# Second layer of a two-layer state-space kernel: eight convolution taps on VectorE, weights by tanh instead of sigmoid, short pieces read out of whole chunks; output stages with earlier loads and two square roots

## The chip, the cores and the metric

The kernel runs on one core of one Trainium2 chip, in fp32. The metric is the device time of one launch in microseconds (us). Engines are named as in the profile: PE is TensorE's matmul, PEld its weight load, DVE VectorE, ACT ScalarE, POOL GpSimd, SP the queue that issues most transfers.

## The reference, cut to what matters

The input is four images of 64x64 pixels with 192 channels. Two layers follow each other, both with 384 inner channels and 16 states. The first layer is a selective scan in four directions, with a layer norm, a gate silu(z), an output matmul and a residual. The change leaves all of it but its output stage alone. The second layer is a 3x3 depthwise convolution with a silu, and four scans of a different form:

```
xc = silu(depthwise_conv3x3(x_val) + conv_b)
dt = softplus(dt @ W_dt + b_dt)
log_dA = dt * A                              # A = -exp(A_log), per channel and state
log_decay = cumsum(log_dA)
decay = exp(log_decay)
h = decay * cumsum(dt * B * u / (decay + 1e-12))
y = sum over states of h * C, plus u * D     # rows, rows backward, columns, columns backward
out = x + (layernorm(y1 + y2 + y3 + y4) * silu(z)) @ W_out
```

A decay falls without limit along a row of pixels, so that a state's part of y is zero in fp32 from some pixel on. The weight decay / (decay + 1e-12) in the scans equals sigmoid(log_decay + ln 1e12), and it equals (1 + tanh((log_decay + ln 1e12) / 2)) / 2.

## The kernel before, in words

**Sizes.** An image is L = 4096 pixels, in NCH = 8 chunks of LC = 512; ND = 3 groups of 128 inner channels; KD = 4 directions; NJ = 4 blocks of 128 pixels in a chunk; NS = 16 states.

**Order of the whole.** The four images go through the first layer one after the other, each with its own projection, scans and output stage. Then the second layer takes all four together through `project`, `prepare`, `scans` and `finish`, each stage in full before the next. `finish` is one function for both layers: it is called four times with one image, and once with four.

**Who orders the instructions.** In both layers' scans the order on PE, ACT, DVE and POOL is written out by hand; SP's is set by a scheduler. In `project`, `prepare` and `finish` a scheduler orders all engines, bounded by the buffers of each pool.

**The output stage** (`finish`, from line 853). For each image, `stats` loads eight y tiles (L870 on), takes mean and variance of each pixel on DVE (L875, L876), and after all eight one square root on ACT and one reciprocal (L878, L879) for all 32 groups of 128 pixels. Then for each of eight tiles: load of the gate zg (L887), Silu on ACT (L888), load of the residual xl, normalisation of four blocks on DVE (L894), 12 transposes on PE (L901) into PSUM, read by ACT with gamma and beta into v (L904), the product v·zg on POOL (L907), 12 output matmuls on PE (L912; each shows as two records), the residual added on DVE (L915) and a store (L916). After the fifth tile of an image the next image's `stats` begin.

**Projection of the second layer** (`project`, from line 1005). For each image and channel group: in-projection matmuls into pad (L1040); for each half of the image, tap 0 on ACT (L1052), tap 1 on ACT into a tile of its own (L1053), their sum on POOL (L1054), and taps 2 to 8 on DVE (L1056), each 128x2048. Then a silu on ACT (L1057); six copies on POOL of the first pixels of each direction into uc (L1064, L1067); 16 matmuls by the diagonal D (L1074), their copies on ACT (L1078) and stores to y. At the image's end uc is stored (L1084), and the gate is projected and stored (L1088).

**What is scanned** (classes, line 947). Since decays end early, a direction's first 256 pixels are enough for state 0, 128 for states 1 to 3, 64 for states 4 to 7 and 32 for states 8 to 15. So each image has chunks of 512 columns for the four directions together: M (the first 128 pixels of each direction), E (the next 128, state 0 only), and two short pieces of M: S (first 64) and Q (first 32). Backward directions have theirs at the other end. A test for the limits leads to a full-length second path, which is not executed with these inputs.

**Preparation** (`prepare`, from line 1092). For M and then E of each image: load uc (L1189), three matmuls to xd (L1192, L1194), three to dp (L1110), softplus as max(dp, 0) + ln(1 + exp(-|dp|)): Abs and Exp on ACT (L1117, L1118), four POOL steps over 128x1536 (L1121, L1122, L1123, L1125), Ln on ACT between (L1124), the sum on DVE (L1127) with dp computed again. Then cumulative sums of dt, the test, e = dt·u (L1199), and `keep` (from L1163), which stores to DRAM: C's rows, B turned, e turned, dt and cum. For the short pieces POOL copies parts of dt, cum, e and of xd into small tiles (L1212, L1215), and `keep` is called for each of them too.

**Scans** (`scans`, from line 1219). Nine items per image: four of M with one state each, two of S with two states side by side, one of E, two of Q with four states. An item is: weights by Sigmoid on ACT (L1254) from cum, decays by Exp on ACT (L1267) from dt, B's product on ACT (L1287), x turned back on PE (L1302), x times weight (L1309) and the scan (L939) on DVE, times C on POOL (L1325), and the sum over states into PSUM by PE (L1343). Sigmoid and Exp lie in different tables of ACT, so weights are made in bursts of five and four items, with a table load before and after (L1254, L1410). Chunks of the next image are loaded at items 3, 5, 6 and 9. At item 2 of the next image the sums of an image are read out (L1369) and added to y in DRAM by DMAs with an add, issued by POOL (L1377, L1380).

Of the kernel before, what the change touches and what calls it, by code (L numbers as in the profile page):

```python
# [10 lines left out]
F32 = mybir.dt.float32  # L11
# [8 lines left out]
LC = 512  # L20
# [382 lines left out]
class FirstLayer:  # L403
# [449 lines left out]
    def finish(self, batches):  # L853

        nc, tc = self.tc.nc, self.tc
        with ExitStack() as ctx:
            pool = lambda name, bufs, **k: ctx.enter_context(tc.tile_pool(name=name, bufs=bufs, **k))
            py, pl, ps, pw = pool("fy", 12), pool("fl", 3), pool("fs", 2), pool("fw", 2)
# [6 lines left out]
            def stats(y):  # L865

                yts = []
                mv = ps.tile([128, NCH * NJ, 2], F32, name="mv")
                for t in range(NCH):
                    yt = py.tile([128, NJ, DI], F32, name="yt")  # L870
                    nc.sync.dma_start(yt, pos(y, t))
                    yts.append(yt)
                    st = pw.tile([128, NJ, nc.vector.BN_STATS_DIM], F32, name="st")
                    for j in range(NJ):
                        nc.vector.bn_stats(st[:, j, :], yt[:, j, :])  # L875
                        nc.vector.bn_aggr(mv[:, t * NJ + j, :], st[:, j, :])  # L876
                rs = ps.tile([128, NCH * NJ], F32, name="rs")
                nc.scalar.activation(rs, mv[:, :, 1], AF.Sqrt, bias=self.ln_eps)  # L878
                nc.vector.reciprocal(rs, rs)  # L879
                return yts, mv, rs  # L880

            ready = stats(batches[0][2])
            for b, (src, dst, _, gate) in enumerate(batches):
                yts, mv, rs = ready
                for t in range(NCH):
                    zg = pl.tile([128, ND, LC], F32, name="zg")
                    nc.sync.dma_start(zg, gate[t])  # L887
                    nc.scalar.activation(zg, zg, AF.Silu)  # L888
                    xl = pl.tile([128, NJ, CH], F32, name="xl")
                    nc.sync.dma_start(xl, pos(src, t))  # L890
                    yt = yts[t]
                    for j in range(NJ):
                        i = t * NJ + j
                        nc.vector.tensor_scalar(  # L894
                            yt[:, j, :], yt[:, j, :], mv[:, i, 0:1], rs[:, i : i + 1], ALU.subtract, ALU.mult
                        )
# [10 lines left out]
                    nc.gpsimd.tensor_tensor(v, v, zg, ALU.mult)  # L907
# [9 lines left out]
                    if t == NCH // 2 and b + 1 < len(batches):  # L917
                        ready = stats(batches[b + 1][2])


class Chunk:
# [3 lines left out]
    def __init__(self, name, width, dram, b):  # L925
        self.name, self.width = name, width
        kept = {"dt": [128, ND, width], "cum": [128, ND, width], "dtuT": [128, width // 128, DI]}
        kept |= {"bT": [128, width // 128, NS], "rows": [NS, width]}
        self.dram = {n: dram.tile(shape, F32, name=f"{n}{name}{b}") for n, shape in kept.items()}
# [12 lines left out]
class SecondLayer(FirstLayer):  # L942
# [6 lines left out]
    def __init__(self, tc, ctx, consts, w, dram, alive):  # L949
# [18 lines left out]
        nc.vector.tensor_scalar_mul(self.A, self.A, -1.0)  # L968
        self.A_max = wp.tile([128, len(self.CLASSES), ND], F32, name="A_max_s")
# [8 lines left out]
        nc.vector.memset(self.ln_q, LN_1E12)  # L978
# [13 lines left out]
    def run(self, batches):  # L992
# [4 lines left out]
        for b, uc in enumerate(ucs):  # L997
            kinds = (("M", LC), ("E", LC), ("S", LC // 2), ("Q", LC // 4))
            chunks.append([Chunk(name, width, self.dram, b) for name, width in kinds])
# [5 lines left out]
    def project(self, batches):  # L1005
        nc, tc = self.tc.nc, self.tc
        with ExitStack() as ctx:
# [17 lines left out]
            for b, (_, y, gate, uc_dram) in enumerate(batches):  # L1025
# [7 lines left out]
                for e in range(ND):  # L1033
# [12 lines left out]
                    for q in range(2):  # L1046
# [6 lines left out]
                        nc.scalar.activation(u, part(1), AF.Identity, scale=weight(1))  # L1053
                        nc.gpsimd.tensor_tensor(acc, acc, u, ALU.add)  # L1054
                        for tap in range(2, 9):
                            nc.vector.scalar_tensor_tensor(acc, part(tap), weight(tap), acc, ALU.mult, ALU.add)  # L1056
# [4 lines left out]
                        for r in range(2):  # L1061
                            k, row = (0, r * n) if q == 0 else (2, nh - (r + 1) * n)
                            to = uc[:, r, e, k * SEG : (k + 1) * SEG].rearrange("p (h w) -> p h w", w=HW)
                            nc.gpsimd.tensor_copy(to, u[:, row : row + n, :])  # L1064
                            for k, col in ((1, r * n), (3, HW - (r + 1) * n)):
                                to = uc[:, r, e, k * SEG : (k + 1) * SEG].rearrange("p (w h) -> p w h", h=HW)
                                nc.gpsimd.tensor_copy(to[:, :, q * nh : (q + 1) * nh], wide[:, col : col + n, :])  # L1067
# [24 lines left out]
    def prepare(self, ucs, batches):  # L1092
        nc, tc = self.tc.nc, self.tc
        with ExitStack() as ctx:
# [63 lines left out]
            def starts(t, n):  # L1158

                v = t.rearrange("... (h k w) -> ... h k w", h=2, w=SEG)  # L1160
                return [v[..., 0, :, :n], v[..., 1, :, SEG - n :]]

            def keep(chunk, xd, tiles):  # L1163

                nb = chunk.width // 128
                nc.sync.dma_start(chunk.dram["rows"], xd[48:64, : chunk.width])
                bp = ps_x.tile([128, NJ, NS], F32, name="bp", tag="xp")
                for j in range(nb):
                    nc.tensor.transpose(bp[:, j, :], xd[32:48, j * 128 : (j + 1) * 128], ident[32:48, 32:48])
                bT = p3.tile([128, NJ, NS], F32, name="bT")  # L1170
                nc.vector.tensor_copy(bT[:, :nb], bp[:, :nb])
                nc.sync.dma_start(chunk.dram["bT"], bT[:, :nb])
                dtuT = p2.tile([128, NJ, DI], F32, name="dtuT")
                for j in range(nb):
                    tp = ps_t.tile([128, DI], F32, name="tp")
                    for d in range(ND):
                        nc.tensor.transpose(
                            tp[:, d * 128 : (d + 1) * 128], tiles["e"][:, d, j * 128 : (j + 1) * 128], ident
                        )
                    nc.scalar.copy(dtuT[:, j, :], tp)  # L1180
                nc.sync.dma_start(chunk.dram["dtuT"], dtuT[:, :nb])
                for name in ("dt", "cum"):
                    nc.sync.dma_start(chunk.dram[name], tiles[name][:, :, : chunk.width])

            for uc_dram, (main, ext, *parts) in zip(ucs, batches):
                before = None
                for r, chunk in enumerate((main, ext)):
# [15 lines left out]
                    tiles = {"dt": dt, "cum": cum, "e": e}  # L1203
                    keep(chunk, xd, tiles)
                    for part in parts if r == 0 else ():
                        n = part.width // KD
                        own = {}
                        for name, t in tiles.items():
                            own[name] = p2.tile([128, ND, LC // 2], F32, name=f"{name}_p")
                            for to, of in zip((slice(0, 2 * n), slice(2 * n, 4 * n)), starts(t, n)):  # L1210
                                to = own[name][:, :, to].rearrange("p d (k w) -> p d k w", w=n)
                                nc.gpsimd.tensor_copy(to, of)  # L1212
                        xo = p2.tile([NX, LC // 2], F32, name="xd_p")
                        for to, of in zip((slice(0, 2 * n), slice(2 * n, 4 * n)), starts(xd[32:64], n)):
                            nc.gpsimd.tensor_copy(xo[32:64, to].rearrange("p (k w) -> p k w", w=n), of)  # L1215
                        keep(part, xo, own)


    def scans(self, batches, ys):
        nc, tc = self.tc.nc, self.tc  # L1220
        with ExitStack() as ctx:
            pool = lambda name, bufs, **k: ctx.enter_context(tc.tile_pool(name=name, bufs=bufs, **k))
            p1, p2, p3, p4, p6 = (pool(f"s{b}", b) for b in (1, 2, 3, 4, 6))
# [15 lines left out]
            def load(it):  # L1239
                for name, shape in (("dt", [128, ND]), ("cum", [128, ND]), ("dtuT", [128]), ("bT", [128])):  # L1240
                    t = p1.tile(list(it.dram[name].shape), F32, name=f"{name}{it.name}")
                    nc.sync.dma_start(t, it.dram[name])
# [4 lines left out]

            def weight(g):

                it, states, _ = flat[g]  # L1250
# [307 lines left out]
```

## Time and profile before

| | us |
|---|---|
| median of 3 runs (lowest, highest) | 11562.15 (11552.21, 11568.8) |
| profiled execution, its span | 11574.44, 11572.7 |
| four images of the first layer, each | about 2484 |
| of this the output stage, first load to last store | 90.3, 86.8, 89.9, 89.8 |
| second layer's projection, first tap to last | 10003.2 to 10617.6 |
| its preparation | 10640 to 10875 |
| its scans | 10875 to 11262 |
| its output stage | 11264 to 11573 |
| DVE, ACT, PE, POOL busy over the span | 84%, 84%, 83%, 79% |
| granted TensorE clock, mean | 0.924 |

A row of an instruction group gives: line, engine, operation, out<-in, partitions x elements, count; then busy us and mean ns of one; then the engine's idle time just before them and what ended most of it. "A<-B" in that last part reads: the engine waited for line B's engine. A row by window gives each engine's busy time, the granted clock, the share of the DMA engines' time and GB/s.

### The profile page before, as it was taken

How to read it: one execution, taken by the hardware profiler on the slowest of the kernel's cores; microseconds unless marked ns; L12 is line 12 of the kernel's file. 1: busy time of each engine (PE TensorE's matmuls, PEld its weight loads, DVE VectorE, ACT ScalarE, POOL GpSimd, SP SyncE). 2: the span in 40 equal slices, each digit the busy share in tenths (PEclk: the TensorE clock that was granted, in tenths of full speed). 3: DMA queues.
4: the chain of work that ended last, by engine and by line, in shares of the span. 5: the costliest groups of instructions: out<-in, count | busy, mean ns of one | idle time of the engine just before them, and what ended most of it. 6: DMA issues, size and time to landing. Idle time of an engine off the chain costs nothing. (4 is left out here: it accounts for less than half of the span.)

```text
span 11572.7 us, 172113 instructions
## 1 busy us (share of the span) xinstructions
PE 9631.2 (83%) x61497; PEld 7333.9 (63%) x61497; DVE 9684.7 (84%) x11675; ACT 9692.9 (84%) x16786; POOL 9137.6 (79%) x3024
## 2 busy tenths in 40 slices
PE   8998888878988888779988888789888888677567
PEld 4776666656776666657766666557766666444346
DVE  4999899957999899939998999669998999675456
ACT  5999999948999999849999999579999999454564
POOL 3999899937999899829998999559998999454444
PEclk8999999988999999989999999889999999887688
DMA  4433344444333344443333444443333443423446
GB/s 124 108 104 100 93 100 100 97 138 111 111 103 95 96 100 99 112 133 109 108 99 93 100 98 100 125 125 107 102 100 94 99 100 92 128 97 127 145 121 224
DMA packets 802422, 1277.16 MB, mean 110 GB/s; under 512 B 56954, under 2 KB 485511, under 8 KB 801044
## 3 DMA queue, kind: packets, MB, share of 16 engines
q1 hardware_dynamic: 796692, 1259.76, 39.6%
q0 software_dynamic: 4864, 6.29, 0.4%
q8 instruction: 489, 8.01, 0.3%
q14 instruction: 377, 3.09, 0.1%
HBM read 958.19 MB, written 307.69 MB: 109 GB/s over the span
## 5 line engine op out<-in xcount | busy, mean ns | idle before, releaser
L738 POOL TENSOR_TENSOR h<-h,bct 128x1536 f32<-128x1536 f32 x2048 | 7061.9, 3469 | 586.4 <-DVE carry L734 483.1
L724 DVE TENSOR_TENSOR_SCAN h<-a,carry,x 128x512 f32<-128x512 f32 x5376 | 6605.2, 1266 | 233.2 <-PE x L716 188.4
L716 PE MATMUL x<-ident,xT 128*128 128x128 f32 x24576 | 4004.7, 287 | 814.4 <-DVE h L724 712.9
L699 ACT ACTIVATE xT<-dtuT,bT 128x384 f32<-128x384 f32 x8192 | 4357.6, 609 | 94.7 <-PE x L716 89.6
L716 PEld LDWEIGHTS x<-ident,xT 128*128 128x128 f32 x24576 | 2807.3, 145 | 2139.4 <-DVE h L724 926.0
L711 ACT ACTIVATE a<-dt,A_log_f 128x512 f32<-128x512 f32 x6144 | 3976.5, 715 | 0.0
L751 PE MATMUL yp<-ident,h 128*128 128x128 f32 x24576 | 3705.9, 277 | 9.2 <-POOL h L738 9.1
L751 PEld LDWEIGHTS yp<-ident,h 128*128 128x128 f32 x24576 | 2946.4, 144 | 78.8 <-issue 63.6
L615 PE MATMUL dp<-xd,w_dtb_f 13*128 13x512 f32 x1536 | 889.9, 663 | 208.9 <-DVE dt L644 207.8
L724 DVE TENSOR_TENSOR_SCAN h<-a,x 128x512 f32<-128x512 f32 x768 | 899.2, 1207 | 195.2 <-PE x L716 117.6
L628 POOL TENSOR_SCALAR wl<-e 128x1536 f32<-128x1536 f32 x128 | 189.2, 1478 | 702.7 <-ACT e L624 379.5
L490 PE MATMUL pp<-xT,w_in 96*128 96x512 f32 x1152 | 551.7, 631 | 27.6 <-ACT pad L1040 26.2
L907 POOL TENSOR_TENSOR v<-v,zg 128x1536 f32<-128x1536 f32 x64 | 238.2, 3742 | 422.2 <-ACT v L904 380.3
L1056 DVE SCALAR_TENSOR_TENSOR acc<-pad,conv_w_s,acc 128x2048 f32<-128x2048 f32 x168 | 446.2, 2702 | 139.1 <-POOL acc L1054 138.8
L615 PEld LDWEIGHTS dp<-xd,w_dtb_f 13*128 13x128 f32 x1536 | 238.7, 192 | 453.9 <-DVE dt L644 336.6
L745 PE MATMUL yp<-yold,ident 128*128 128x512 f32 x768 | 444.0, 663 | 72.6 <-DMA yold<-y 72.6
L621 ACT ACTIVATE e<-dp 128x512 f32<-128x512 f32 x384 | 224.7, 585 | 311.3 <-DVE dt L644 141.8
L641 POOL TENSOR_TENSOR e<-e,wl 128x1536 f32<-128x1536 f32 x128 | 444.9, 3476 | 0.3
L638 POOL TENSOR_TENSOR e<-e,dt 128x1536 f32<-128x1536 f32 x128 | 442.5, 3457 | 0.3
L490 PEld LDWEIGHTS pp<-xT,w_in 96*128 96x128 f32 x1152 | 227.5, 203 | 295.5 <-issue 253.9
L912 PE MATMUL op<-w_out,v 128*128 128x192 f32 x1536 | 302.0, 364 | 105.9 <-POOL v L907 104.3
L734 DVE TENSOR_REDUCE carry<-h 128x3 f32<-128x3 f32 x2048 | 322.7, 158 | 70.4
(180 smaller groups left out, 7053.6 us busy)
## 6 DMA issues: line engine op xcount, KB each, us to landing
bct<-xp SPq DMA_DIRECT2D x1024, 512.0 KB, 5.0
uT<-uT SPq DMA_DIRECT2D x64, 768.0 KB, 4.8
yold<-y SPq DMA_DIRECT2D x64, 768.0 KB, 8.0
y<-yt SPq DMA_DIRECT2D x64, 768.0 KB, 4.2
uT<-uT SPq DMA_DIRECT2D x128, 384.0 KB, 5.0
yold<-y SPq DMA_DIRECT2D x128, 384.0 KB, 5.4
y<-yt SPq DMA_DIRECT2D x128, 384.0 KB, 4.6
yt<-y SPq DMA_DIRECT2D x64, 768.0 KB, 7.9
```

What stands on the lines that cost most here:

```text
L490: self.tc.nc.tensor.matmul(pp, self.w_in[:, i, e * 128 : (e + 1) * 128], self.xT[:, i, t * LC : (t + 1) * LC], start=(i == 0), stop=(i == ...
L615: nc.tensor.matmul(self.dp[d], w, self.xd[0 : DR + 1, :], start=True, stop=True)
L638: nc.gpsimd.tensor_tensor(self.e, self.e, self.dt, ALU.subtract)
L641: nc.gpsimd.tensor_tensor(self.e, self.e, self.wl, ALU.add)
L699: nc.scalar.mul(xTs[g][:, j, :], it.dtuT[:, j * DI : (j + 1) * DI], it.bT[:, j, n : n + 1])
L711: nc.scalar.activation(as_[g][:, d, :], it.dt[:, d, :], AF.Exp, scale=scale)
L716: nc.tensor.transpose(xs[g, d][:, j * 128 : (j + 1) * 128], xTs[g][:, j, d * 128 : (d + 1) * 128], ident)
L724: nc.vector.tensor_tensor_scan(along(hs[g][:, d, :], it.k), along(as_[g][:, d, :], it.k), along(xs.pop((g, d)), it.k), 0.0 if it.first els ...
L738: nc.gpsimd.tensor_tensor(hs[g], hs[g], bc(cs[g - n % 2][:, n % 2, :], 1, ND), ALU.mult)
L745: nc.tensor.matmul(it.yp[b], ident, yo, start=True, stop=False, skip_group_check=True)
L751: nc.tensor.matmul(it.yp[b][:, i * 128 : (i + 1) * 128], hs[g][:, d, j * 128 : (j + 1) * 128], ident, start=False, stop=n == NS - 1, is_tr ...
L1056: nc.vector.scalar_tensor_tensor(acc, part(tap), weight(tap), acc, ALU.mult, ALU.add)
```

## The change

It has four parts.

1. **Output stages.** `start` issues the loads of y and of the gate in turn, with the Silu of each gate tile; the gate has ten buffers of its own. Statistics, square root and reciprocal are split: tiles 0 and 1, then 2 to 7. Normalisation moves to POOL, all of it inside `start`; the product v·zg moves to DVE. `start` for the next image is called where `stats` was.
2. **Projection.** Tap 1 becomes a DVE tap; ACT's tap 1 and POOL's add go. The six copies into uc move from POOL to ACT.
3. **Preparation.** Only M and E are prepared and kept. POOL's copies and the short pieces' `keep` are gone. B turned is stored with a factor 0.5.
4. **Scans.** Weights by Tanh, with A and ln 1e12 halved, and the scan's first step is (tanh + 1)·x in one DVE instruction. Tanh and Exp share one table, loaded once; each item's weight is made one item ahead, beside its decay. For items of four states, three POOL multiplies of 128x512 by A come first, and one ACT instruction over 128x1536 instead of twelve. The chunks S and Q are read in pieces from M's arrays in DRAM: for dt and cum six transfers each, for e turned and B four each; C's rows by four. The chunks of the next image are loaded at items 4, 6, 7 and 8, three buffers hold weights (six before) and five hold h (four before). PE adds the first item of an image at item 3, and the read-out follows the scans of item 2.

Core of the diff (lines are after.py's and before.py's without numbers):

```diff
-            py, pl, ps, pw = pool("fy", 12), pool("fl", 3), pool("fs", 2), pool("fw", 2)
+            py, pz, pl, ps, pw = pool("fy", 10), pool("fz", 10), pool("fl", 3), pool("fs", 2), pool("fw", 3)
...
+            def start(y, gate):
+                yts, zgs = [], []
                 for t in range(NCH):
                     yt = py.tile([128, NJ, DI], F32, name="yt")
                     nc.sync.dma_start(yt, pos(y, t))
                     yts.append(yt)
+                    zg = pz.tile([128, ND, LC], F32, name="zg")
                     nc.sync.dma_start(zg, gate[t])
                     nc.scalar.activation(zg, zg, AF.Silu)
+                    zgs.append(zg)
+                for lo, hi in ((0, 2), (2, NCH)):
...
+                    nc.scalar.activation(rs, mv[:, :, 1], AF.Sqrt, bias=self.ln_eps)
+                    nc.vector.reciprocal(rs, rs)
+                    for t in range(lo, hi):
+                        for j in range(NJ):
+                            i = (t - lo) * NJ + j
+                            part = yts[t][:, j, :]
+                            nc.gpsimd.tensor_scalar(part, part, mv[:, i, 0:1], rs[:, i : i + 1], ALU.subtract, ALU.mult)
...
-                    nc.gpsimd.tensor_tensor(v, v, zg, ALU.mult)
+                    nc.vector.tensor_mul(v, v, zg)
...
-                        nc.scalar.activation(u, part(1), AF.Identity, scale=weight(1))
-                        nc.gpsimd.tensor_tensor(acc, acc, u, ALU.add)
-                        for tap in range(2, 9):
+                        for tap in range(1, 9):
                             nc.vector.scalar_tensor_tensor(acc, part(tap), weight(tap), acc, ALU.mult, ALU.add)
...
-                            nc.gpsimd.tensor_copy(to, u[:, row : row + n, :])
+                            nc.scalar.copy(to, u[:, row : row + n, :])
...
-                                nc.gpsimd.tensor_copy(to[:, :, q * nh : (q + 1) * nh], wide[:, col : col + n, :])
+                                nc.scalar.copy(to[:, :, q * nh : (q + 1) * nh], wide[:, col : col + n, :])
...
-                nc.vector.tensor_copy(bT[:, :nb], bp[:, :nb])
+                nc.vector.tensor_scalar_mul(bT, bp, 0.5)
...
+            def by_state(g, of, to, func, scale=1.0, bias=0.0):
                 it, states, _ = flat[g]
+                w = HALF // len(states)
+                if len(states) == 4:
+                    lo, hi = states[0], states[-1] + 1
+                    for d in range(ND):
+                        nc.gpsimd.tensor_tensor(
+                            halves(to[:, d, :]).rearrange("p h (n w) -> p h n w", w=w),
+                            bc(halves(of[:, d, :]), 2, hi - lo),
+                            bc(bc(self.A[:, 0, d, lo:hi], 1, 2), 3, w),
+                            ALU.mult,
+                        )
+                    nc.scalar.activation(to, to, func, scale=scale, bias=bias)
+                    return
...
+            def weight(g):
+                sg[g] = p3.tile([128, ND, LC], F32, name="sg")
+                by_state(g, flat[g][0].cum, sg[g], AF.Tanh, 0.5, self.ln_q)
...
-                nc.vector.tensor_mul(x, x, sg[g][:, d, :])
+                nc.vector.scalar_tensor_tensor(x, sg[g][:, d, :], 1.0, x, ALU.add, ALU.mult)
...
-                    for at, i in ((3, 0), (5, 2), (6, 1)):
+                    for at, i in ((4, 0), (6, 2), (7, 1), (8, 3)):
...
-                    burst = {3: range(g + 1, g + 6), 8: range(g + 1, g + 5)}.get(n, ())
...
                     if g + 1 < N:
+                        weight(g + 1)
                         decay(g + 1)
...
-                        end_y(b - 1)
...
                     if g < N:
                         c_product(g)
+                    if n == LAG and b > 0:
+                        end_y(b - 1)
```

In the changed kernel the lines that the prediction names stand here: normalisation L891, gate load L873, v·zg L911, taps L1094, copies into uc L1102 and L1105, diagonal matmuls L1112, POOL's multiplies by A L1273.

## The prediction

> **What bounds the kernel now.** I read the spans by stage first, because the change leaves the first layer alone up to its output stages (some 2395 us per image): what it can win lies in the windows below. In order: the last 90 us of a first-layer image (its output stage), then the second layer's projection, preparation, scans and output stage. Columns: busy time and instructions of each engine, granted TensorE clock, DMA share, GB/s.
>
> ```profile
> 9856.00:9946.00 90.00, 50.61 (x288) 48.04 (x288) 43.48 (x145) 32.29 (x37) 30.02 (x8) 0.78 0.63 208
> 10003.00:10618.00 615.00, 462.91 (x1726) 270.32 (x1725) 480.16 (x246) 328.49 (x396) 334.87 (x201) 0.86 0.31 101
> 10640.00:10875.00 235.00, 141.45 (x315) 65.39 (x314) 72.50 (x200) 84.64 (x108) 107.00 (x96) 0.59 0.37 136
> 10885.00:11223.00 338.00, 220.16 (x1437) 176.54 (x1438) 209.92 (x362) 289.71 (x583) 152.21 (x72) 0.81 0.42 109
> 11264.00:11573.00 309.00, 207.32 (x1153) 194.29 (x1153) 189.93 (x519) 118.59 (x136) 118.01 (x32) 0.83 0.70 234
> ```
>
> Only the scans have an engine near full (ACT, 290 of 338). Elsewhere no engine reaches 80%, so chains of waits set the time, and I read who waits for whom. Groups of the projection:
>
> ```profile
> L1056 DVE SCALAR_TENSOR_TENSOR acc<-pad,conv_w_s,acc 128x2048 f32<-128x2048 f32 x168 | 446.2, 2702 | 139.1 <-POOL acc L1054 138.8
> L1054 POOL TENSOR_TENSOR acc<-acc,u 128x2048 f32<-128x2048 f32 x24 | 134.6, 5608 | 130.9 <-ACT u L1053 130.9
> L1064 POOL COPY uc<-u 128x128 f32<-128x128 f32 x46 | 102.1, 2219 | 179.2 <-ACT u L1057 179.2
> L1067 POOL COPY uc<-u 128x64 f32<-128x64 f32 x91 | 102.4, 1152 | 0.0
> ```
>
> VectorE's 615 us are 446 of taps plus 139 of waiting for POOL's tap add. The reader should see two costs of POOL here: the wait, and the mean of 2702 ns against a shortest tap of 2271 and a longest of 6609. The small copies, too, have a mean far above their shortest (about 290 ns). In the preparation, chain and rows are:
>
> ```profile
> L1127 DVE SCALAR_TENSOR_TENSOR dt<-dp,e 128x512 f32<-128x512 f32 x24 | 15.1, 683 | 65.6 <-POOL e L1125 65.6
> L1123 POOL TENSOR_TENSOR e<-e,dt 128x1536 f32<-128x1536 f32 x8 | 27.4, 3423 | 0.7
> L1121 POOL TENSOR_SCALAR wl<-e 128x1536 f32<-128x1536 f32 x8 | 11.8, 1470 | 31.1 <-ACT e L1118 24.3 <-issue 6.8
> ```
>
> The first two images of the scans, columns as above:
>
> ```profile
> 10885.00:10969.00 84.00, 45.85 (x254) 35.56 (x254) 52.00 (x90) 83.85 (x163) 27.59 (x8) 0.72 0.47 153
> 10969.00:11053.00 84.00, 57.53 (x390) 46.24 (x390) 52.91 (x91) 70.89 (x144) 41.35 (x21) 0.84 0.48 119
> ```
>
> VectorE's waits in the scans (us, times, longest) name ACT's decays:
>
> ```profile
> DVE h L939 <- ACT a L1267: 46.3, 8, 13.0
> ```
>
> Groups of the last output stage:
>
> ```profile
> L912 PE MATMUL op<-w_out,v 128*128 128x192 f32 x768 | 156.1, 371 | 54.5 <-POOL v L907 53.0 <-DVE ot L915 1.5
> L907 POOL TENSOR_TENSOR v<-v,zg 128x1536 f32<-128x1536 f32 x32 | 118.0, 3706 | 179.3 <-ACT v L904 137.5 <-ACT zg L888 35.8 <-PE vp L901 6.0
> L894 DVE TENSOR_SCALAR yt<-yt,mv,rs 128x384 f32<-128x384 f32 x128 | 81.2, 692 | 0.1
> ```
>
> Per tile, evacuation, POOL product and output matmul follow one another, and all tiles of an image wait for one square root behind all eight loads and statistics.
>
> **A. First-layer output stages, four times.** Now: first load to last store 90.3, 86.8, 89.9 and 89.8 us, mean 89.2. In image 4 statistics end 22 us after the first load and eight tiles take 14.6 us a pair. After: y and gate loads alternate, 16 tiles of 786 KB at 2.1 us each (375 GB/s, the rate this burst reaches now), so the last lands at +36 and the second statistics and root end at +40. Tiles 0 and 1 lie under this. Six remain: each 12 transposes (starts 0.109 us apart: 1.3 us) and 24 output matmuls (0.1625: 3.9 us), 5.2 us of PE, and about 1 us of waiting, as the tiles go in groups of three: 37.5 us. With 4 us for last add and store, and two more table changes (1.28 us each, one exposed), +83. Gain 6 us, four times: **−25** (0 to −50). The zg loads and Silus, which I cost at nothing more, hide under the y loads' own waits; uncovered they would cost 8 × 1.48 = 12 us per image.
>
> **B. Projection.** Tap 1 leaves ACT and POOL and becomes a VectorE tap; POOL keeps only memsets. 48 taps per image at a start-to-start of 2.298 us give 110.3 us, statistics 10, small work 4, and a gap at the image boundary, 26 to 28 us now while the pipeline restarts, taken as 23 without the wait for POOL: 147 per image, against 162.5 now (42 taps = 96.5, 16 or so lengthened taps, 8 of gaps, 26 to 28, 14). ACT loses 24 × 2.0 us and gains 144 copies of 0.25 to 0.48 us (35 to 69; no ACT row of 64 to 128 columns, so bounded by the overhead seen in a 128x128 Exp, 386 ns, and a 128x384 copy, 477): about even, at 330 of 553 us. Counted from today's start (A's gain is in A): 10003 + 3×147 + 112 (the last image has no boundary and ends with its taps) = 10556 against 10617.6, **−62** (−40 to −90).
>
> Here the Trainium skill's page "SBUF — State Buffer" (Who interferes with whom) decides whether lengthened taps go: a VectorE instruction with two SBUF inputs and a GpSimd one that reads SBUF exclude each other for a whole instruction. Taps of up to 6.6 us beside adds of 4.5 to 5 fit it. By this rule the output stage gets worse: v·zg, moved to VectorE, has two SBUF inputs and runs beside POOL's normalisations. By the row of a VectorE product of the same size (e = dt·uc, 1.74 to 2.06 us) a tile costs VectorE 1.9; by the rule add POOL's 4 × 0.45 in series, 3.7 us. Both stay under the 6.7 us of a tile in E, so I take no loss.
>
> **C. Preparation.** Only whole chunks are kept; 28 us of POOL copies, ten piece stores per image, and their PE transposes go. Products start 10663.4 to 10859.4: 196 us for seven steps, alternately some 22 us (M to E, with about 2 to 3 us of copies between POOL's steps) and 35 (E to M, since the next uc load stands in SP's queue behind E's store of cum). After, SP's order puts that load behind M's stores, so the step is the chain: dp matmuls and Exp 7.4, POOL 1.47+1.47+3.42+3.42, the Ln between with its table change, delta and dp restart 2.8, about 20.4. Seven: 143, **−53**; the first product 9 us sooner after the last tap (SP's order), another 4.6 where Ln waits for xd today. Together −67; as the chain at 20.4 is nearly free of slack, I take **−60** (−40 to −75).
>
> **D. Scans.** Sixteen table loads (20.5 us) and the bursts of weights go; Tanh shares the table with Exp. ACT per image: 4 M items × 6.2, E 7.8, 2 S × 7.6, 2 Q × 5.1 (two passes of 1.48 over 1536 columns and b 2.1) = 58 us, 71 now. VectorE: 9 × 5.88 and E's extra, about 57. POOL: nine products at 3.45, twelve store issues near 1.0, and 12 new 128x512 multiplies. Those have no row: linear from the 128x1536 product they cost 1.15; at twice that, because the operands are broadcast, 2.3. I take 1.25: 15 us, sum 58. At Q items the multiplies stand ahead of an h·c product in POOL's queue, and y matmuls wait for it; five h buffers cover 7.5 us. Now the bound engine's 71 becomes 84; the same ratio gives 58 × 1.18 = 68.5. First scan 17.5 us after the first load instead of 24.8: −7. Three periods and a shorter last: −53. **−60** (−10 with multiplies at 2.3 us, to −80). Moving end_y behind the next image's scans delays only stores. Pieces S and Q now come by 40 DMAs per image in 256 B and 128 B runs. "DMA: Bandwidth & Descriptors" (Specifications) asks for 512 B or more, which speaks against it. By the trace a 256 B packet takes 18 ns and a 128 B one 13, against 27 for 512 B: 3072 of each over 16 engines are 6 us per image, DMA share 0.47 there, loaded items ahead: hidden. If they doubled, 6 us once an image at the worst.
>
> **E. Last output stage.** 309 us now, from the last scan some 350. After: loads begin under the last scans; first op waits for y stores (end L+28, L the last scan), loads, root and POOL's normalisations (no row with per-partition scalars; 0.37 by the immediate form's 1470/4, 0.9 at a tensor product's rate; I take 0.45, near the first, the same operation): L+46. Then 32 tiles. PE needs 5.2, DMA 53.4 us per image or 6.7: DMA bounds. 46 + 214 + 10 = 270: **−80** (−45 to −105).
>
> Sum −25 −62 −60 −60 −80 = −287. The profiled execution took 11574.4 (span 11572.7), 12 above the runs' median 11562.2; its sum is 11287, on the median's basis 11275.
>
> **Rivals.** (1) *In-order PE becomes the bound.* Its projection work is about 454 us at full clock, now wanted in 553; at the 0.86 granted it needs 528. Against: it overlaps taps today. For: 0.59 to 0.86 clocks. B falls to −30, C to −50, E to −40, sum −205: 11357. (2) *POOL bounds the scans* with multiplies at 2.3 us: 31+12+28 = 71 per image, × 1.18 = 84: D only −10, 11325. (3) *Slower:* normalisations on POOL with two per-partition scalars are slow, 256 in all. Each output tile hides up to 1.65 us each (6.7/4). Beyond this every us costs 64 × 4 us; the 287 are gone at 1.65 + 1.12 = 2.8 us, and at 3.5 us the time is 11275 + 474 = 11749. Against: twice the slowest bound from the rows.
>
> **How the numbers follow.** Forecast 0.62; PE 0.15; POOL in scans 0.17; slower 0.025; the rest, that parts cancel within 0.2% (about what a measurement of this kernel can tell from no change), 0.015 and a further gain 0.02. Range: the far ends of A to E lie 113 below the sum, not reached together; 70% of it gives 11196. Above, the PE rival with 23 more, 11380, which takes in POOL in the scans too.
>
> **What would show it.** A: last store by +83 of first load, tiles 0 and 1 before the second root. B: no tap above 2.5 us, no wait for POOL, first to last tap 553 us; PE waits in L1112 would speak for rival 1. C: 20 us between deltas, uc load ahead of E's stores. D: one table load, period below 70; the multiply's mean at L1273 decides rival 2. E: 6.7 us per tile, DMA share near 0.8; L891's mean decides rival 3. Wrong wholly if first-layer scans move.

## The result, and the profile after

The changed kernel takes 11400.9 us (median of 4 runs, 11396.0 to 11404.0), against 11563.9 for the kernel before (4 runs): a ratio of 0.986, 95% interval 0.9843 to 0.9877. It is faster by 163 us, which the interval sets clear of no change; 287 were forecast, and the time lies 21 us above the stated range.

The profiled spans differ by 173.8 us (11572.7 and 11398.9). Marks that both traces share split it. Each part runs from the mark before it to its own (kernel before, then changed kernel, in us); the last two columns are the change:

| part | ends at | forecast | measured |
|---|---|---|---|
| A first-layer output stages | first tap: 10003.2, 10006.2 | -25 | +3 |
| B projection | last tap: 614.3, 522.4 | -62 | -92 |
| C preparation | last step of softplus on VectorE: 242.5, 189.4 | -60 | -53 |
| D scans | last item's multiply on VectorE: 359.9, 339.3 | -60 | -21 |
| E last output stage | end: 352.8, 341.7 | -80 | -11 |

Stages of the changed kernel, by window, columns as in the prediction: the last first-layer output stage, projection, preparation, scans, last output stage.

```profile
9860.00:9963.00 103.00, 57.18 (x288) 50.80 (x288) 45.25 (x125) 37.65 (x41) 58.34 (x32) 0.69 0.52 179
10006.00:10528.00 522.00, 467.56 (x1758) 276.22 (x1756) 471.36 (x270) 320.67 (x522) 5.24 (x40) 0.92 0.38 121
10528.00:10718.00 190.00, 134.50 (x293) 56.15 (x292) 65.69 (x177) 82.72 (x104) 78.73 (x32) 0.62 0.40 142
10746.00:11057.00 311.00, 213.32 (x1414) 175.29 (x1413) 209.43 (x359) 222.96 (x383) 199.16 (x120) 0.83 0.48 113
11085.00:11393.00 308.00, 208.15 (x1153) 191.14 (x1153) 168.17 (x427) 137.57 (x153) 240.85 (x131) 0.79 0.72 246
```

A first-layer output stage now takes 100 to 103 us from its first y load to its last store, where the prediction had 90 before and 83 after. POOL went from 30 to 58 us in it, and from 118 to 241 in the last stage. The last stage's groups say with what:

```profile
L891 POOL TENSOR_SCALAR yt<-yt,mv,rs 128x384 f32<-128x384 f32 x128 | 238.3, 1874 | 45.5 <-DVE rs L886 32.3 <-DVE ot L919 13.2
L905 PE MATMUL vp<-ident,yt 128*128 128x128 f32 x384 | 71.7, 331 | 96.8 <-POOL yt L891 95.2 <-ACT v L908 1.3
L916 PE MATMUL op<-w_out,v 128*128 128x192 f32 x768 | 140.2, 348 | 3.5 <-DVE ot L919 3.1 <-DVE mv L883 0.4
```

A normalisation takes 1.87 us on the mean, 7.5 per tile of four, and PE's transposes wait 95 us for it. The output matmuls, which waited 53 us for POOL's product before, now wait 3.5 us in all. In the projection:

```profile
L1094 DVE SCALAR_TENSOR_TENSOR acc<-pad,conv_w_s,acc 128x2048 f32<-128x2048 f32 x192 | 439.2, 2343 | 52.6 <-ACT acc L1092 51.9
L1105 ACT COPY uc<-u 128x64 f32<-128x64 f32 x96 | 24.4, 304 | 0.0
L1102 ACT COPY uc<-u 128x128 f32<-128x128 f32 x48 | 14.2, 296 | 0.1
```

24 more taps cost VectorE less busy time than before, none is over 2.36 us, and VectorE never waits for POOL. In the preparation the steps follow each other by 19 to 21 us, the three from E to the next image's M among them; only M to E takes 29 us in the second and the fourth image. There PE's transposes of M's e, which wait for VectorE, stand ahead of E's dp matmuls. In the second image:

```profile
10605.70 2.79 PE L1209 MATMUL tp<-ident,e 128*128 128x128 f32 x12 [10.66 <-DVE dt L1232]
10608.42 8.04 PE L1148 MATMUL dp<-xd,w_dtb_s 13*128 13x512 f32 x9
```

In the scans, ACT's waits (us, times, longest):

```profile
ACT sg L1279 <- POOL sg L1273: 54.2, 8, 13.4
ACT ytm L1392 <- PE yp L1366: 20.4, 3, 8.7
```

The period, from the first multiply on VectorE of one image to that of the next, is 82 and 84.5 us for the second and third image (86 and 85 before), though ACT's work is 57 us per image. ACT now stands behind POOL's multiplies, once for 13.4 us though three of them take about 3.5. POOL's own queue, while the second image is scanned, in order of time, shows what else is in it:

```profile
10813.93 1.08 POOL L1400 DMA_DIRECT2D y<-yte  x1 [4.89 <-ACT yte L1384]
10818.32 1.69 POOL L1403 DMA_DIRECT2D y<-yte  x2 [3.31 <-DMA y<-yte]
10822.60 0.90 POOL L1400 DMA_DIRECT2D y<-yte  x1 [2.59 <-ACT xT L1314]
10826.50 1.69 POOL L1403 DMA_DIRECT2D y<-yte  x2 [2.99 <-DMA y<-yte]
10827.63 10.79 POOL L1348 TENSOR_TENSOR h<-h,bct 128x1536 f32<-128x1536 f32 x3
...
10845.02 0.90 POOL L1400 DMA_DIRECT2D y<-ytm  x1
10850.08 1.69 POOL L1403 DMA_DIRECT2D y<-ytm  x2 [4.15 <-DMA y<-ytm]
10856.73 0.90 POOL L1400 DMA_DIRECT2D y<-ytm  x1 [4.95 <-DMA y<-ytm]
10860.72 1.68 POOL L1403 DMA_DIRECT2D y<-ytm  x2 [3.09 <-DMA y<-ytm]
10861.84 10.78 POOL L1348 TENSOR_TENSOR h<-h,bct 128x1536 f32<-128x1536 f32 x3
10872.04 3.56 POOL L1273 TENSOR_TENSOR sg<-cumQ,A_log_s 128x512 f32<-128x512 f32 x3
```

Stores that add to y (L1400, L1403) keep POOL's queue for 14 us and again for 17: those of one region of y are issued 0.3 to 0.6 us after those of the region before have landed. Three products pile up behind each time, and behind the second pile stand the multiplies that ACT needs for the next weight. The same stretches of stores stand in the kernel before (15 and 16 us), but there no weight or decay of ACT waits for POOL.

### The profile page after: what moved, and what is told of

Same layout as the page of the kernel before. It is cut to its first block, busy times and chain, and to the rows that moved or that the text cites. A ratio compares the mean times of both kernels' runs of the same rounds, so it can differ in the third digit from the quotient of the medians.

```text
span 11398.9 us, 171795 instructions
## 1 busy us (share of the span) xinstructions
PE 9629.2 (84%) x61449; PEld 7328.0 (64%) x61449; DVE 9660.8 (85%) x11508; ACT 9638.7 (85%) x16730; POOL 9049.1 (79%) x3032
## 5 line engine op out<-in xcount | busy, mean ns | idle before, releaser
L891 POOL TENSOR_SCALAR yt<-yt,mv,rs 128x384 f32<-128x384 f32 x256 | 466.9, 1837 | 200.1 <-DVE rs L886 187.0
L1094 DVE SCALAR_TENSOR_TENSOR acc<-pad,conv_w_s,acc 128x2048 f32<-128x2048 f32 x192 | 439.2, 2343 | 52.6 <-ACT acc L1092 51.9
L905 PE MATMUL vp<-ident,yt 128*128 128x128 f32 x768 | 163.6, 361 | 305.4 <-POOL yt L891 303.6
```

Of the source, the lines that this page charges most:

```text
L891: nc.gpsimd.tensor_scalar(part, part, mv[:, i, 0:1], rs[:, i : i + 1], ALU.subtract, ALU.mult)
```

## The experiments

Two theories: the price of one POOL normalisation sets the output stages (A and E), and the stores in POOL's queue hold the scans (D). The rivals: in the output stages the loads, or the chain from the second square root, set the pace whoever normalises; in the scans ACT waits for products that wait for the scans, stores or not. The ratios below are to the kernel before, timed anew beside each group of runs (medians of 11551 to 11557 us).

**Who normalises.**

```diff
-nc.gpsimd.tensor_scalar(part, part, mv[:, i, 0:1], rs[:, i : i + 1], ALU.subtract, ALU.mult)
+nc.vector.tensor_scalar(part, part, mv[:, i, 0:1], rs[:, i : i + 1], ALU.subtract, ALU.mult)
```

> The changed kernel with the 256 normalisations on VectorE instead of POOL. Theory (one POOL normalisation with two per-partition operands takes 1.64 us at the least, 6.6 to 7.4 us per tile, and this sets the pace of the output stages): the last tiles of a first-layer image no longer wait for it, about -15 us in each of four images; in the last stage VectorE has 7.7 us of work per tile (statistics 2.7, normalisation 1.8, product 1.8, adds 1.4) against 8.7 us between stores now, about -25; together about -85, 11315 us. Rival (the 16 alternating loads or the chain from the second square root set the pace whoever normalises): less than -30, above 11370.

Measured: 11268.7 us, ratio 0.9754 (0.9738 to 0.9771). One takes 0.475 us (shortest, median and longest in ns; the changed kernel's first, then this run's):

```profile
L891 POOL TENSOR_SCALAR yt<-yt,mv,rs x256: 1636/1643/4062, 2413.3 to 11374.4; 128x384 f32<-128x384 f32 x128
L891 DVE TENSOR_SCALAR yt<-yt,mv,rs x256: 466/475/492, 2410.4 to 11211.9; 128x384 f32<-128x384 f32 x128
```

The first tap comes at 9916.5 instead of 10006.2, and E takes 298.5 instead of 341.7; B, C and D are as in the changed kernel. The theory holds, with a larger gain than it said, and the rival falls.

With constants in place of mean and reciprocal, which leaves the layer norm out:

```diff
-nc.gpsimd.tensor_scalar(part, part, mv[:, i, 0:1], rs[:, i : i + 1], ALU.subtract, ALU.mult)
+nc.gpsimd.tensor_scalar(part, part, 0.0, 1.0, ALU.subtract, ALU.mult)
```

> The normalisations stay on POOL but with constants 0 and 1 in place of mean and reciprocal, so that the layer norm is left out; the statistics and roots are still made. Theory (the per-partition operands are what cost): one takes 0.4 to 0.6 us as the constant form over 1536 columns (1.47 us) says, POOL falls out of the path, about -20 in each first-layer image and -50 in the last stage: -130, about 11270. Rival (a POOL instruction on 384 columns has a price of its own, with whatever operands): it stays near 1.6 us and the time stays within 20 us of 11400.

Measured: 11296.2 us, ratio 0.9779 (0.9763 to 0.9795), but one still takes 1.50 us. So the operands aren't what costs: the theory fails, and the rival is right on the price, though not on the time. The gain has a reason that I had overlooked: without mean and root in it, the normalisation no longer waits for them. In the changed kernel it waited 45.5 us before these 128, mostly for the reciprocal; here, in the last stage:

```profile
L891 POOL TENSOR_SCALAR yt<-yt 128x384 f32<-128x384 f32 x128 | 209.1, 1666 | 17.4 <-DVE st L882 17.4
```

The run can't tell the price from the wait. The next one measures the price by itself.

**Twelve forms of the POOL instruction**, six times each, ahead of everything, on tiles that nothing else uses:

```diff
+for _ in range(6):
+    nc.gpsimd.tensor_scalar(part, part, 0.0, 1.0, ALU.subtract, ALU.mult)
+for _ in range(6):
+    nc.gpsimd.tensor_scalar(part, part, 0.0, 1.0, ALU.add, ALU.mult)
...
```

> The changed kernel with 72 POOL instructions put ahead of everything, on tiles of their own: six each of twelve forms of the same two-operation instruction (subtract and multiply, or add and multiply; constants or per-partition operands; in place or not; 384 or 1536 columns; and a multiply alone). With constants the normalisation still took 1.49 us for 384 columns, as much as add and multiply takes for 1536 (1.47), so the operands aren't the price. Theory (subtract is done by a slow path of some 3.9 ns per column, add by one of 0.96): the forms with subtract take 1.5 to 1.65 us at 384 and about 6 us at 1536, those with add 0.4 to 0.5 and 1.47. Rival 1 (writing onto the operand is slow): split by in place or not. Rival 2 (384 columns have a floor near 1.5 us): all forms near 1.5 us, and 1.5 at 1536 too. Time about 70 us longer at the start, which counts for nothing.

Shortest, median and longest in ns, by line. In order: subtract and multiply with constants, add and multiply with constants, the same two with per-partition operands (all in place, 384 columns); subtract and add with constants, add with operands, into another tile; then 1536 columns: subtract and add in place; subtract, and add with operands, into another tile; last, a multiply alone by an operand.

```profile
L1473 POOL TENSOR_SCALAR fbig<-fbig x6: 1495/1497/1879, 2.7 to 11.0; 128x384 f32<-128x384 f32 x6
L1475 POOL TENSOR_SCALAR fbig<-fbig x6: 511/511/511, 12.6 to 15.5; 128x384 f32<-128x384 f32 x6
L1477 POOL TENSOR_SCALAR fbig<-fbig,fs x6: 1645/1646/1647, 16.2 to 24.9; 128x384 f32<-128x384 f32 x6
L1479 POOL TENSOR_SCALAR fbig<-fbig,fs x6: 661/661/661, 26.6 to 30.4; 128x384 f32<-128x384 f32 x6
L1481 POOL TENSOR_SCALAR fto<-fbig x6: 1495/1496/1497, 31.2 to 39.1; 128x384 f32<-128x384 f32 x6
L1483 POOL TENSOR_SCALAR fto<-fbig x6: 510/511/511, 40.7 to 43.6; 128x384 f32<-128x384 f32 x6
L1485 POOL TENSOR_SCALAR fto<-fbig,fs x6: 660/660/661, 44.2 to 48.0; 128x384 f32<-128x384 f32 x6
L1487 POOL TENSOR_SCALAR fbig<-fbig x6: 5378/5378/5380, 48.8 to 76.1; 128x1536 f32<-128x1536 f32 x6
L1489 POOL TENSOR_SCALAR fbig<-fbig x6: 1470/1471/1471, 81.6 to 89.3; 128x1536 f32<-128x1536 f32 x6
L1491 POOL TENSOR_SCALAR fto<-fbig x6: 5378/5379/5380, 90.9 to 118.2; 128x1536 f32<-128x1536 f32 x6
L1493 POOL TENSOR_SCALAR fto<-fbig,fs x6: 1620/1620/1621, 123.7 to 132.3; 128x1536 f32<-128x1536 f32 x6
L1495 POOL TENSOR_SCALAR fbig<-fbig,fs x6: 1237/1242/1249, 134.0 to 140.7; 128x384 f32<-128x384 f32 x6
```

From 384 to 1536 columns subtract grows by 3.37 ns per column ((5378 - 1496) / 1152), add by 0.83. Per-partition operands add 0.15 us whatever the width; in place or not makes no difference. Both rivals fall. (The time, 11530 us in a single run, is 130 longer than the changed kernel's, about the stretch that these rows span.)

**The same normalisation without a subtraction.**

```diff
+nm = ps.tile([128, n], F32, name=f"nm{lo}")
+nc.vector.tensor_scalar_mul(nm, mv[:, :, 0], -1.0)
...
-nc.gpsimd.tensor_scalar(part, part, mv[:, i, 0:1], rs[:, i : i + 1], ALU.subtract, ALU.mult)
+nc.gpsimd.tensor_scalar(part, part, nm[:, i : i + 1], rs[:, i : i + 1], ALU.add, ALU.mult)
```

> The changed kernel with the normalisation still on POOL and still with per-partition operands, written as (y + (-mean)) * r, with -mean made by one small VectorE instruction per root. If subtract is the price: the instruction falls to about 0.5 us, the output stages are bound as in the version with VectorE, and the time is 11260 to 11290. If it is writing in place or the 384 columns: it stays at 1.64 us, and 11400 us within 10.

Measured: 11280.8 us, ratio 0.9758 (0.9741 to 0.9774); one takes 0.66 us:

```profile
L893 POOL TENSOR_SCALAR yt<-yt,nm,rs x256: 650/660/3920, 2414.0 to 11239.9; 128x384 f32<-128x384 f32 x128
```

Of the 132 us between the changed kernel and the version on VectorE, 120 come back with the normalisation still on POOL. The engine was no problem; the operation was.

**On ACT** (r·y - mean·r as one activation):

```diff
+nm = ps.tile([128, n], F32, name=f"nm{lo}")
+nc.vector.scalar_tensor_tensor(nm, mv[:, :, 0], -1.0, rs, ALU.mult, ALU.mult)
...
-nc.gpsimd.tensor_scalar(part, part, mv[:, i, 0:1], rs[:, i : i + 1], ALU.subtract, ALU.mult)
+nc.scalar.activation(part, part, AF.Identity, bias=nm[:, i : i + 1], scale=rs[:, i : i + 1])
```

> The changed kernel with the normalisation on ACT, as r * y + (-mean * r). ACT has 36 to 47 of 75 us busy in the last stage with the normalisation on VectorE, VectorE 63 to 70; so in the last stage VectorE is relieved by 1.9 us per tile and ACT takes 4 times about 0.6. Theory (VectorE and DMA share the bound there): 10 to 30 us below the version on VectorE, 11245. Rival (ACT's order, with eight Silus and two table changes ahead of the normalisations, delays them): 0 to 40 us above it.

Measured: 11358.6 us, ratio 0.9829 (0.9812 to 0.9845): 90 us above the version on VectorE. The rival holds, by more than twice what it said: one takes 0.69 us, and in the first-layer stage PE's transposes wait 33.5 us for ACT's normalisations. What in ACT's order delays them was not taken apart.

**What the rest of the output stage's change brings**, each taken back from the version on VectorE. The product on POOL again:

```diff
-nc.vector.tensor_mul(v, v, zg)
+nc.gpsimd.tensor_tensor(v, v, zg, ALU.mult)
```

> The version with the normalisation on VectorE (11269 us), and the product v*zg back on POOL: the engines of the kernel before, with the early loads and two roots of the changed one. VectorE gets 1.8 us per tile free, POOL takes 3.44. Theory (lock: VectorE's normalisations, 0.475 us alone, 0.69 on the mean beside POOL's product in the kernel before, are held up, and each tile's path is 1.6 us longer): 10 to 40 us slower, 11280 to 11310. Rival (VectorE, 65 to 70 of 75 us busy in the last stage, is what sets it): 10 to 20 us faster, 11250 to 11260.

Measured: 11369.9 us, ratio 0.984 (0.9824 to 0.9857): 101 us slower, two and a half times the most that I expected; 66 lie before the first tap, 40 in E. That POOL's product holds up VectorE's normalisations isn't the main cause, since their mean in E is only 0.513 us. The path through a product of 3.43 us for 1.75 is 1.7 us longer per tile, which for 64 tiles is 108, near the 101. But the first layer's 32 tiles lose more than their share and those of E less, so how the path adds up stays open.

```diff
-for lo, hi in ((0, 2), (2, NCH)):
+for lo, hi in ((0, NCH),):
```

> The version with the normalisation on VectorE (11269 us), with one square root for all eight tiles instead of two. Theory (the first root lets tiles 0 and 1 run under the loads of the others): each first-layer output stage 6 to 9 us longer (77 now), the last stage 5 to 10 at its start, 30 to 45 in all, about 11305. Rival (PE and the loads' end set the stage anyway): less than 10.

Measured: 11341.3 us, ratio 0.9822 (0.9805 to 0.9838): 73 us slower. A first-layer stage takes 95 us from the first y load instead of 77, and the first store of E comes 98 us after the last multiply of the scans instead of 67. The theory's sign holds; the second root is worth about double.

**The scans: y stores spread out.**

```diff
-nc.gpsimd.dma_start(ys[b][lo : lo + SEG, :], y[:, k, :], accum_op=ALU.add)
+late.append([(ys[b][lo : lo + SEG, :], y[:, k, :])])
...
+def store_one():
+    for to, of in late.pop(0) if late else ():
+        nc.gpsimd.dma_start(to, of, accum_op=ALU.add)
...
 if n == LAG and b > 0:
     end_y(b - 1)
+store_one()
...
```

> The changed kernel with the y stores of the second layer's scans spread out: after each item's product on POOL the stores of one region are issued instead of all four regions in a row. Theory (each store waits in POOL's queue for the one before to land, 14 to 16.5 us per chunk of y, and products, the multiplies by A and then ACT's tanh stand behind it): the gap of 18.7 us after item 2 and that of 15.9 us after item 6 shrink, the image period goes from 83 to about 72, -40 us in all: 11360. Rival (ACT waits for the multiplies because these stand behind products that wait for the scans, stores or not): less than -12.

Measured: 11369.5 us, ratio 0.984 (0.9823 to 0.9856). The period is 69.3 and 70.3 us, where 68.5 was forecast, and D takes 301.1 us, 58.8 less than in the kernel before. The gap after item 2 of the second image, from its first multiply on VectorE to that of item 3, fell from 18.7 to 9.7, that after item 6 from 15.9 to 10.0. Same view of ACT's waits:

```profile
ACT sg L1279 <- POOL sg L1273: 36.4, 8, 6.6
ACT a L1279 <- POOL a L1273: 11.2, 8, 1.4
```

The wait for PE's sums is gone; the rest, 4.6 us each time, is near what three multiplies take by themselves. (This trace's gain in D is 38 us; the median's is 31.)

**Items of four states without POOL's multiplies** (twelve ACT instructions, as in the kernel before):

```diff
-if len(states) == 4:
+if len(states) == 5:
```

> The changed kernel with items of four states done as those of two: twelve ACT instructions for weight and decay, no multiplies on POOL. ACT gets 10 us more per image (58 to 68 of 83), POOL 8.6 us less. Theory (ACT stalls behind POOL's queue: 54 us of waits in 329): the gap after item 6 falls from 15.9 to under 9 us, the items of four states take 10 us each; no net loss, -20 to +5. Rival (ACT's own work sets the scans): +30 to +40.

Measured: 11378.1 us, ratio 0.9847 (0.9831 to 0.9864), D 317.1 us in the trace, 22 less than in the changed kernel. The gap after item 6 is 10.9 instead of 15.9, and the two Q items take 5.9 and 7 us. The theory holds: the multiplies, meant to relieve ACT, cost more in POOL's queue than ACT gained.

**Together.** VectorE normalises (first edit above) and the stores are spread:

> Normalisation on VectorE and the y stores of the second layer's scans spread out, together. If the two costs lie on paths of their own, the gains add: 132 and 31 below the changed kernel, about 11237 us. If one covers part of the other, above 11255.

Measured: 11233.5 us, ratio 0.9721 (0.9705 to 0.9738). The gains add; it beats both kernels.

The same without the multiplies:

> Normalisation on VectorE, y stores spread (11233 us together), and the items of four states by twelve ACT instructions, without POOL's multiplies. With the stores spread the multiplies no longer stand behind them. Theory (what the multiplies cost was their place behind the stores): no gain is left, and ACT's 10 us more per image show: period 70 to 73, 11235 to 11250. Rival (two sets of multiplies of 3.5 us stand in ACT's path whatever is ahead of them; the Q items take 10.0, 11.1 and 8.0 us with the stores spread): period 66 to 68, 11215 to 11225.

Measured: 11233.7 us, ratio 0.9722 (0.9706 to 0.9739). By the trace the period is 67.2 and D takes 8 us less than with the multiplies, as the rival says; the time shows nothing of it, and the runs of either version lie up to 13 us apart. Not settled.

**The projection: copies into uc on POOL again**, all taps on VectorE:

```diff
-nc.scalar.copy(to, u[:, row : row + n, :])
+nc.gpsimd.tensor_copy(to, u[:, row : row + n, :])
...
-nc.scalar.copy(to[:, :, q * nh : (q + 1) * nh], wide[:, col : col + n, :])
+nc.gpsimd.tensor_copy(to[:, :, q * nh : (q + 1) * nh], wide[:, col : col + n, :])
```

> The changed kernel with the six copies into uc back on POOL; all eight taps stay on VectorE. Theory (a POOL instruction that reads SBUF and a tap exclude each other): a good part of the taps over 2.5 us comes back, none being there now, and the projection takes 535 to 555 us instead of 522; 11415 to 11435 us. Rival (what lengthened the taps was the 128x2048 add alone, and the copies cost ACT 30 to 70 us now): 515 to 522, 11395.

Measured: 11500.9 us, ratio 0.9949 (0.9932 to 0.9965): 100 slower than the changed kernel, the projection 605.6 us. Something is shut out, but the other way round from what I expected: no tap is over 2.38 us, and the copies are long.

```profile
L1102 POOL COPY uc<-u x48: 283/293/36513, 10042.6 to 10632.0; 128x128 f32<-128x128 f32 x48
L1094 DVE SCALAR_TENSOR_TENSOR acc<-pad,conv_w_s,acc x192: 2278/2343/2379, 10010.7 to 10613.9; 128x2048 f32<-128x2048 f32 x192
```

```profile
ACT acc L1092 <- POOL pad L1077: 97.4, 4, 29.0
```

A copy of 0.29 us lasts up to 36.5: each of the four longest lies beside 16 taps that follow one another without a break, and ends with them. The borders of the next pad are set on POOL behind the copies, and ACT waits 97 us for them. Taken back alone, the copies cost 83 of B's 92 us; the move of tap 1 was not taken back alone. The rival was right on the taps: all 15 taps over 2.5 us in the kernel before lie beside POOL's 128x2048 add. It was wrong that the copies on POOL cost nothing.

## Why the prediction was wrong

**The failed step is the price of the normalisation in E and A**, "0.37 by the immediate form's 1470/4, 0.9 at a tensor product's rate; I take 0.45, near the first, the same operation". It is not the same operation: line 1121 adds and multiplies, this one subtracts and multiplies. It takes 1.64 us alone (1.84 on the mean of 256), 3.6 times what I took, and above both ends of my bounds. Rival 3 named the right instruction; I gave it 0.025, because the wrong row bounded it.

Rival 3's own sum failed as well, at "each output tile hides up to 1.65 us each". By it 1.84 us would have cost 0.19 x 256 = 49 us, not the 132 that the version on VectorE saves. The normalisations aren't spread under the tiles' pace: they can't start before their root. In the first image's stage POOL stands idle from 26 to 43 us after the first y load, until the second root, and then runs 24 in a row to 86 us; the last store is issued at 100.6. With add in place of subtract the 24 end at 57 us and the last store is issued at 78.7.

With the price removed (the version on VectorE) the time is 11269 us, where 11275 was forecast. That agreement is in part luck, by the parts of that run against the kernel before: A -87 (forecast -25), B -93 (-62), C -54 (-60), D -21 (-60), E -54 (-80).

- **A** was undersized: with a cheap normalisation a stage takes 77 us from its first load, not 83, and the second root shortens a stage by 18. About 8 us more per image have a cause that my sum did not contain: the first loads of what follows are now issued before the stage's last store (8 us before it in the first image; 3 us after it in the kernel before), so its in-projection starts some 26 us after the last output matmul instead of 32 to 35. This also makes up for most of the 10 to 14 us by which the changed kernel's stages are longer.
- **B** was right that the lengthened taps and the wait for POOL's add go. It was undersized at the image boundary: between the last tap of an image and the first of the next lie 13 to 14 us, where I took 23. Taps start 2.26 us apart (median), where I took 2.298. Beside the add, which lasted 5.0 to 7.1 us there and not 4.5 to 5, POOL delayed the taps; beside the copies the taps delay POOL, and that my sum did not contain. Rival 1, PE as the bound, did not come about: it saw B at -30, with a granted clock of 0.86, and the clock was 0.92.
- **C** holds: five of seven steps take 19 to 21 us, and those from E to M, which the uc load's earlier place was to shorten by 15 us, are 15 us shorter. What I left out is PE's order, by which two steps from M to E take 29.
- **D** failed at "twelve store issues near 1.0". The multiplies' price was right (1.04 us alone; 1.42 on the mean where they overlap one another; I took 1.25), and so was the period once the stores are spread (69 to 70 against 68.5). The issues take about 1 us each, as said, but with the waits between them they keep POOL's queue for 14 and 17 us per image instead of 12 in all, and this holds ACT once its weights come from there; five h buffers don't cover it. What the waits cost in the kernel before no run shows. This is rival 2's bound with another cause. The pieces read from DRAM stayed hidden, as said: waits for them show only at the first image.
- **E** without the slow operation takes 298.5 us, not 273: its first store comes 67 us after the last multiply, where I had 46, and the 31 stores behind it follow by 7.3 us each, where I had 6.7. In the second of its windows DMA is busy 0.95 and VectorE 70 of 75 us; which of the two sets the pace is not shown, as the run that moved work from VectorE to ACT was held up there:

```profile
11080.00:11155.00 75.00, 55.09 (x324) 51.15 (x322) 69.93 (x187) 43.73 (x48) 0.00 (x0) 0.88 0.95 331
```

The normalisations' mean, 1.84 us, lies above their 1.64 because 47 of the 256 took longer than 1.7 us, and each of these 47 lies beside a product v·zg on VectorE. This is what the Trainium skill's page "SBUF — State Buffer" (Who interferes with whom) states: a VectorE instruction with two SBUF inputs contends with a GpSimd instruction that reads SBUF. It spoke against the product on VectorE. In the changed kernel the product still takes 1.72 to 2.18 us; it is POOL's side that grew. With the normalisation on VectorE, and so no POOL in the stage, the product takes 1.75 and its place on VectorE is worth 101 us; with the normalisation on POOL its place was not tested.

## What to carry to other kernels

A row prices an instruction only if it has the same operation, not just the same opcode and shape: where a new instruction has no such row, measure it by itself before moving 256 of them. Before another engine is made to depend on a queue, look for the waits in that queue which that engine didn't have to sit through before, such as transfers that wait for one another; spread them out. And where two engines hold each other up, look at which of them runs without a break: here it was not delayed, and the short instructions of the other one waited.

## What the runs showed of the hardware

- On POOL, subtract-and-multiply on fp32 costs 3.37 ns per column (5.378 us at 1536 columns, 1.496 at 384) and add-and-multiply 0.83 (1.471 and 0.511); per-partition operands add 0.15 us. A multiply alone by a per-partition operand took 1.24 us on 384 columns, more than add and multiply together (0.66). VectorE does subtract and multiply on the same tile in 0.475 us. With two tensors as inputs, POOL's subtraction isn't slower than its addition: 3.43 and 3.42 us on 128x1536 (L1161 and L1163 of the changed kernel).
- A POOL copy of 0.29 us lasted up to 36.5 us beside back-to-back VectorE instructions with two SBUF inputs, none of which took longer than 2.38 us. Beside POOL's add of 128x2048, the same VectorE instructions took up to 6.61 us.
